# Two-layer graph network on one core: how the experts' gathered rows are turned

## The chip, the core and the metric

The kernel runs on one core of one Trainium2 chip. The metric is the device time of one execution in microseconds (us). The kernel before took 1842.46 us (median of three runs, 1840.32 to 1843.58). The engines are TensorE (PE, whose weight loads are listed apart as PEld), VectorE (DVE), ScalarE (ACT), GpSimd (POOL) and SyncE (SP). Each has an instruction queue of its own, and SP, ACT and POOL also issue DMAs from that queue.

## The reference, cut to what matters

There are N = 3327 nodes with D = 256 features, and a dense 0/1 adjacency matrix. The reference computes four steps, each on a layer norm of the running state `x` and each added to it.

```
x += gat2(layernorm(x), adj)                 # two heads, softmax over neighbours
x += moe(layernorm(x))                       # 16 experts, the best 2 of each node
x += elu(gat1(layernorm(x), adj))            # one head
x += recurrent(layernorm(x))                 # 30 steps: tanh, silu, layernorm, 256x256 matmul

# moe, for a node h and each of its two experts e with weight g_e:
out = sum_e g_e * ((silu(h @ w1[e]) * (h @ w2[e])) @ w3[e])     # w1,w2: 256x512, w3: 512x256
```

All arithmetic is in 32-bit floating point.

## The kernel before, in words

Nodes lie in 26 columns of 128 partitions (`NT` = 26). The program has four stages. First comes the two-head attention, then the experts, then the one-head attention, and last the 30 recurrent steps.

**Attention (`attend`).** The work is cut into parts: a group of columns and a head. The groups of the first attention are columns 0-3, 4-9, 10-15, 16-21 and 22-25, so a part is 512 or 768 wide. For each of the 26 source columns ACT makes `e` (L276), DVE multiplies it by the mask into `pT` (L281), and PE multiplies `pT` with `wh` (L286). `e` and `pT` have three buffers each (pool `edge0`), so ACT and DVE can be a few columns ahead of PE.

**Routing (`route`).** While the next group is being attended to, the finished group is routed in small steps taken from a queue called `later`. DVE measures the rows, POOL takes the power -1/2 (`rstd`, L121), and DVE writes the normalized `row` (L128). One DMA per group, issued from ACT (L516), stores `row` in DRAM as `table_x`. PE transposes `row` in pairs of columns (L148), ACT copies the result out of PSUM (L149), PE makes the gate logits (L526), and DVE picks the two experts and a place in each expert's list (`ati`, L579). POOL then writes the lists with one indirect DMA per column and choice (L592).

**Tiles of the experts.** The lists are cut into tiles of 128 rows of one expert (`find_tiles`). Sixteen tiles are made from the first 16 columns (`FIRST` = 16), and the other 45 once all columns are routed (`ALWAYS` = 61). Tile s uses one of three sets of matrices, number s mod 3. `weights(s)` issues the loads of w1, w2 and w3 from SP (L800 to L802), and skips the transfer if that set already holds the expert. Two of the three sets lie in the memory of `wh`, which becomes free when the attention ends.

**The loop over tiles (`work_off`).** In step s, POOL gathers the rows of tile s+4 from `table_x` by an indirect DMA (L761) into a `rb` buffer that holds three tiles; there are two such buffers, shared with the attention's row factors. PE makes the products with w1 and w2 (L835, `product`), ACT applies silu (L881), DVE multiplies (L885). PE transposes the next tile's rows (`features_first`, L826) and ACT copies them out (L827). Then PE makes the product of tile s-1 with w3 (L851, `results`), DVE weighs it (L854), and POOL scatters it to `given` (L855). The part of the routing that is left over (the group of columns 22-25) runs in the same loop as `aside`.

The order on each engine is fixed when the program is built: a scheduler with its own estimate of times lays the instructions of each engine out in one list. Instructions marked to keep program order are exempt, and so is whatever a dependency ties.

## Time and profile before

| | |
|---|---|
| median of three runs | 1842.46 us (1840.32 to 1843.58) |
| the profiled execution's own time | 1841.14 us |
| its span, first to last instruction | 1839.4 us |
| granted TensorE clock | 0.995 |
| PE busy | 1787.4 us, 97% of the span |
| DVE, ACT, POOL busy | 1319.1, 1223.9 and 888.4 us |
| first attention with the routing, from 92 to 388 us | PE busy 289.9 of 296 us, DMA share 0.45 |
| experts, from 388 to 741 us | PE busy 346.2 of 353 us, DMA share 0.89 |

A line of the timeline gives the start in us, the busy time in us, the engine, the line of the kernel, the operation, output<-inputs and, after x, how many instructions were merged; in brackets stands how long the engine had been idle and who released it. SPq and ACTq are DMAs issued from those queues. In a group line the last fields are the total busy time, the mean of one in ns, and the idle time before. In the answer by stages each engine has its busy time and, in brackets, its instructions, followed by the granted clock, the share of time the DMA engines were busy, and GB/s.

### The profile page before, as it was taken

Reading aid. Unit: us, or ns where it says so; the run is one execution under the profiler, and the core shown is the slowest. Engines: PE = TensorE matmul, PEld = TensorE weight load, DVE = VectorE, ACT = ScalarE, POOL = GpSimd, SP = SyncE. Lnnn points to the kernel's source line nnn. Section 1 sums busy time; section 2 is a strip of 40 time slices with the busy share of each in tenths; the row PEclk is TensorE's granted clock in tenths of the full one; section 3 lists DMA queues with packets and bytes.
Section 4 is the critical chain, followed back from the end, with each engine's and each line's share of the span. In section 5 each row is a group of like instructions: output and inputs, shape, how many; then the busy total and the mean of one; then the engine's idle time right before and its main releaser. Section 6 shows DMA issues by size and latency. Waiting matters only on the chain.

```text
span 1839.4 us, 32502 instructions
## 1 busy us (share of the span) xinstructions
PE 1787.4 (97%) x10980; PEld 1631.7 (89%) x10980; DVE 1319.1 (72%) x4039; ACT 1223.9 (67%) x1587; POOL 888.4 (48%) x654
## 2 busy tenths in 40 slices
PE   7999999999999999799999999999999999999997
PEld 6999999898999999688888878888888888888886
DVE  6888878853222222657677678999999999999998
ACT  2877667642111111366666579999999999999994
POOL 3010212155333332100111028988898889888984
PEclk9999999999999999899999999999999999999999
DMA  8887360258999886400000036666667666666667
GB/s 178 114 123 91 66 101 16 67 187 255 349 345 333 304 301 225 159 9 22 14 18 22 12 84 172 172 172 168 171 167 178 173 172 172 172 167 169 175 172 218
DMA packets 458610, 284.44 MB, mean 155 GB/s; under 512 B 305269, under 2 KB 418220, under 8 KB 458442
## 3 DMA queue, kind: packets, MB, share of 16 engines
q1 hardware_dynamic: 442322, 249.47, 48.4%
q0 software_dynamic: 11440, 28.09, 8.8%
q10 hardware_dynamic: 4680, 4.76, 0.8%
q8 instruction: 90, 1.47, 0.3%
q14 instruction: 78, 0.64, 0.1%
HBM read 168.19 MB, written 91.69 MB: 141 GB/s over the span
## 4 chain that ended last, share of the span: by engine, by line
PE 67%; issue 10%; DVE 6%; POOL 5%; DMA 3%; ACT 1%; another core or an unknown queue 0%; SPq 0%; POOLq 0%; DVEq 0%; ACTq 0%
PE po L1120 35%; PE acc L286 24%; PE bank L1085 4%; DVE pT L281 3%; POOL given L855 2%; POOL rb L761 2%; DMA given<-wh,to 2%; PE bank L835 1%; PE acc L163 1%; PE bank L148 1%; DMA old<-kept 1%; PE bank L526 1%; PE acc L851 1%; DMA lists<-pair,ati 0%; DVE x L1130 0%
## 5 line engine op out<-in xcount | busy, mean ns | idle before, releaser
L276 ACT ACTIVATE e<-rb,minus,full 128x384 f32<-128x384 f32 (+3 forms) x494 | 399.2, 823 | 168.6 <-DVE pT L281 150.8
L1055 POOL TENSOR_TENSOR th<-th,x 128x1024 f32<-128x1024 f32 (+1 forms) x210 | 465.0, 2214 | 94.1 <-ACT th L1052 86.4
L281 DVE SCALAR_TENSOR_TENSOR pT<-e,part,adjT 128x384 f32<-128x384 f32 (+3 forms) x494 | 383.5, 782 | 117.8 <-PE acc L286 101.9
L1120 PE MATMUL po<-wc,adjT 128*128 128x256 f32 x1888 | 422.2, 379 | 0.0
L1120 PEld LDWEIGHTS po<-wc,adjT 128*128 128x128 f32 x1888 | 356.4, 190 | 47.6 <-DVE x L1130 0.3
L1130 DVE SCALAR_TENSOR_TENSOR x<-po,rr,bb 128x256 f32<-128x256 f32 x780 | 325.1, 478 | 61.8 <-PE po L1120 61.2
L286 PE MATMUL acc<-wh,pT 128*128 128x129 f32 x2704 | 311.0, 276 | 2.3 <-DVE pT L281 2.3
L286 PEld LDWEIGHTS acc<-wh,pT 128*128 128x128 f32 x2704 | 305.5, 192 | 3.6 <-DVE pT L281 3.0
L286 PE MATMUL acc<-s_wh,pT 128*128 128x257 f32 x1352 | 295.5, 381 | 3.6 <-DVE pT L281 3.6
L286 PEld LDWEIGHTS acc<-s_wh,pT 128*128 128x128 f32 x1352 | 255.8, 190 | 42.7 <-DVE pT L281 7.0
L1120 PE MATMUL po<-wc,zT 128*128 128x256 f32 x1232 | 281.0, 379 | 0.8 <-DVE x L1130 0.8
L1064 DVE BATCH_NORM_STATS2 stats<-z 128x6 f32<-128x256 f32 x780 | 274.1, 412 | 1.4 <-ACT z L1059 1.4
L1120 PEld LDWEIGHTS po<-wc,zT 128*128 128x128 f32 x1232 | 229.2, 190 | 29.7 <-issue 1.1
L1095 ACT COPY adjT<-z 128x1024 int16<-128x1024 int16 x236 | 235.2, 1044 | 4.8 <-DVE pT L281 2.0
L121 POOL TENSOR_TENSOR rstd<-ve,neg_half 128x4 f32<-128x4 f32 (+3 forms) x28 | 32.0, 1141 | 410.4 <-DVE ve L119 312.3
L1052 ACT ACTIVATE th<-x 128x1024 f32<-128x1024 f32 (+1 forms) x210 | 209.2, 996 | 29.0 <-DVE x L1130 23.8
L1075 POOL TENSOR_TENSOR rr<-rr,neg_half 128x4 f32<-128x4 f32 (+1 forms) x210 | 206.8, 985 | 26.4 <-DVE rr L1070 26.3
L1059 ACT ACTIVATE z<-th 128x1024 f32<-128x1024 f32 (+1 forms) x210 | 207.0, 986 | 7.9 <-POOL th L1055 1.8
L885 DVE TENSOR_TENSOR pT<-e,bank 128x512 f32<-128x512 f32 x61 | 41.9, 688 | 179.7 <-PE bank L835 119.6
L881 ACT ACTIVATE e<-bank 128x512 f32<-128x512 f32 x61 | 36.4, 597 | 196.9 <-PE bank L835 117.2
L835 PEld LDWEIGHTS bank<-hT,wh 128*128 128x128 f32 x1280 | 149.6, 192 | 9.3 <-issue 4.5
L835 PE MATMUL bank<-hT,wh 128*128 128x128 f32 x1280 | 150.6, 276 | 6.5 <-ACT hT L827 2.5
(196 smaller groups left out, 1546.6 us busy)
## 6 DMA issues: line engine op xcount, KB each, us to landing
wh<-in_w_dram SPq DMA_DIRECT2D x120, 512.0 KB
apart<-adjT SPq DMA_DIRECT2D x236, 256.0 KB
first_set<-in_w_dram SPq DMA_DIRECT2D x63, 512.0 KB
in_bytes<-in_adj_dram POOLq DMA_DIRECT2D x3, 2496.0 KB
adjT<-apart SPq DMA_TRANSPOSE x236
x<-in_x_dram SPq DMA_DIRECT2D x6, 512.0 KB
kept<-x SPq DMA_DIRECT2D x8, 384.0 KB
old<-kept SPq DMA_DIRECT2D x6, 512.0 KB
```

The costliest lines, as they stand in the source:

```text
L276: nc.scalar.activation(e[:, : n * P], rb[:, : n * P], AF.Relu, scale=sc.full[:, j, h : h + 1], bias=sc.minus[:, j, h : h + 1],)
L281: masked = nc.vector.scalar_tensor_tensor(pT[:, : n * P], e[:, : n * P], sc.part[:, j, h : h + 1], adjT[:, j // 2, ts[0] * P : (ts[-1] + 1 ...
L286: nc.tensor.matmul(po[c], lhsT=pT[:, c * P : (c + 1) * P], rhs=wh[:, j, h, :], start=(j == 0 and c % per_bank == 0), stop=(j == NT - 1), s ...
L835: nc.tensor.matmul(p[:, f, :], lhsT=w[:, k, f * P : (f + 1) * P], rhs=hT[:, k, :], start=(k == 0), stop=(k == KD - 1),)
L1052: self.put(nc.scalar.activation(self.th, self.hs, AF.Tanh, scale=1.0 / S))
L1055: self.put(nc.gpsimd.tensor_tensor(self.th, self.th, self.hs, ALU.add))
L1059: self.put(nc.scalar.activation(self.z, self.th, AF.Silu, scale=1.0 / S))
L1064: self.put(nc.vector.bn_stats(stats[:, j, :], self.z[:, j, :]))
L1075: self.put(nc.gpsimd.tensor_tensor(r, r, neg_half[:, : self.n], ALU.pow))
L1095: self.put(nc.scalar.copy(parts[:, c : c + 2], halves[:, c : c + 2]))
L1120: nc.tensor.matmul(self.po[:, j, :], lhsT=self.zT(j, k), rhs=wc[:, k, :], start=(k == 0), stop=(k == KD - 1),)
L1130: nc.vector.scalar_tensor_tensor(self.hs[:, j, :], self.po[:, j, :], self.r[:, j : j + 1], bb, op0=ALU.mult, op1=ALU.add)
```

## The change

The gathered rows of a tile are no longer transposed by TensorE. There are four parts.

1. `table_x` holds each row as two planes of 16-bit halves: all low halves, then all high halves. In `route`, ACT copies each pair of columns into such planes (new L524), in a buffer of the attention's `e` ring, and issues one DMA for each pair (new L526): 13 DMAs where there were 5.
2. After the gather (new L774, same size), a tile is written to one of six DRAM buffers `asked` (`put`, new L782), issued from SP for the first three tiles and from ACT for the others. A transposing DMA from SP (`face`, new L786) brings it back with features on the partitions, into one of three `face` buffers. `features_first`, with its two transposes and one copy for each tile, is gone.
3. The matmuls of `product` and `results` (new L864 and L880) are tied to each other in program order by dependencies without semaphores.
4. Numbers of tiles are dealt so that consecutive tiles of one expert go to the same set of matrices, s, s+3, s+6 and so on, where before they went to s, s+1, s+2.

```diff
-    table_x = dram.tile([NP, D], F32, name="table_x")
+    table_x = dram.tile([NP, 2 * D], I16, name="table_x")
@@ route
-            nc.scalar.dma_start(table_x[here, :].rearrange("(t p) d -> p t d", p=P), row[:, :n, :])
+            halves = row.bitcast(I16).rearrange("p j (d b) -> p j b d", b=2)
             for j0 in range(0, n, 2):
+                planes = run.tile([P, MOST * P], F32, name="e").bitcast(I16)[:, : 4 * D]
+                nc.scalar.copy(planes.rearrange("p (j b d) -> p j b d", j=2, b=2), halves[:, j0 : j0 + 2])
+                here = slice((t0 + j0) * P, (t0 + j0 + 2) * P)
+                nc.scalar.dma_start(
+                    table_x[here, :].rearrange("(t p) c -> p t c", p=P), planes.rearrange("p (j c) -> p j c", j=2)
+                )
                 hT = turned(row[:, j0 : j0 + 2, :], turn, ps)
@@ numbers of tiles
-        numbers(two[:, 0, :], [[1, SLOTS]], 0, 0)
+        for s0, n in ((0, FIRST), (FIRST, ALWAYS - FIRST)):
+            no = 0
+            for lane in range(SETS):
+                here = two[:, 0, s0 + lane : s0 + n : SETS]
+                numbers(here, [[1, here.shape[1]]], no, 0)
+                no += here.shape[1]
@@ gathered
+            ahead.append(rows)
+        def put(queue):
+            put_down.append(next(asked))
+            queue.dma_start(put_down[-1], ahead.popleft())
+        def face():
+            hT = faces.tile([P, KD, P], F32, name="face")
+            nc.sync.dma_start(
+                hT.bitcast(I16), put_down.popleft().rearrange("t (b d) -> (t b) d", b=2), transpose=True
+            )
+            facing.append(hT)
@@ product, results: every matmul through behind_latest
+        def behind_latest(ins):
+            nonlocal latest
+            if latest:
+                tc.add_manual_dep(
+                    ins.ins, latest.name,
+                    mybir.DependencyInfo(mybir.DependencyClass.NoSync, mybir.DependencyReason.DATA),
+                    reason="the experts' products in their order",
+                )
+            latest = ins.ins
@@ work_off
-            hT = features_first(ahead.popleft())
+            hT = facing.popleft()
...
                     nc.scalar.activation(act, pa, AF.Silu)
+                    if s + 3 < s1:
+                        put(nc.scalar)
...
-                        hT = features_first(ahead.popleft())
+                        hT = facing.popleft()
                 if s > max(s0, 1):
                     results(s - 1, hidT)
+                if s + 2 < s1:
+                    face()
                 if s + SETS - 1 < s1:
                     weights(s + SETS - 1)
@@ between attention and experts
-        ahead.append(gathered(3))
+        gathered(3)
+        for _ in range(3):
+            put(nc.sync)
+        face()
         weights(1)
+        face()
```

More of the change, by code (lines that the diff above doesn't have):

```diff
@@ L507, in gat_moe_gat_recurrent_ffn @@
         gate = moe.enter_context(tc.tile_pool(name="gate", bufs=1))
+        faces = moe.enter_context(tc.tile_pool(name="faces", bufs=3))
         turn = moe.enter_context(tc.tile_pool(name="turn", bufs=2))
@@ L514, in route @@
             normalized([x[:, t, :] for t in ts], [row[:, j, :] for j in range(n)])
-            here = slice(t0 * P, (t0 + n) * P)
-            nc.scalar.dma_start(table_x[here, :].rearrange("(t p) d -> p t d", p=P), row[:, :n, :])
+            halves = row.bitcast(I16).rearrange("p j (d b) -> p j b d", b=2)
             yield
@@ L613, in route @@
                 for s in range(3):
-                    ahead.append(gathered(s))
+                    gathered(s)
             if ts is groups0[2]:
@@ L650, in gat_moe_gat_recurrent_ffn @@
         two = rec.tile([P, 2, SLOTS], F32, name="prod")
-        numbers(two[:, 0, :], [[1, SLOTS]], 0, 0)
+        for s0, n in ((0, FIRST), (FIRST, ALWAYS - FIRST)):
[4 more added lines that the diff above has]
+                no += here.shape[1]
+        numbers(two[:, 0, ALWAYS:], [[1, SLOTS - ALWAYS]], ALWAYS - FIRST, 0)
         numbers(two[:, 1, :], [[P, SLOTS]], 2 * NP, 1)
@@ L692, in find_tiles @@
             yield
-            tile_no = two[:, 0, :n]
+            tile_no = two[:, 0, here]
             mine = room_m[:E, :, :n]
@@ L753, in find_tiles @@
             nc.vector.tensor_tensor(to[:, here], tof, spare, ALU.add)
-        places = []
+        places, asked = [], cycle([dram.tile([P, 2 * D], I16, name=f"asked{q}") for q in range(6)])
+        ahead, put_down, facing = deque(), deque(), deque()
         def gathered(s):
@@ L759, in gathered @@
                 places.append(rows_p.tile([P, MOST * P], F32, name="rb"))
-            row = places[-1][:, (s % 3) * D : (s % 3 + 1) * D]
+            rows = places[-1].bitcast(I16)[:, (s % 3) * 2 * D : (s % 3 + 1) * 2 * D]
             nc.gpsimd.indirect_dma_start(
-                out=row, out_offset=None, in_=table_x[: EARLY * P, :] if s < FIRST else table_x,
+                out=rows, out_offset=None, in_=table_x[: EARLY * P, :] if s < FIRST else table_x,
                 in_offset=bass.IndirectOffsetOnAxis(ap=which[:, s : s + 1], axis=0),
             )
-            return row
+            ahead.append(rows)
[8 more added lines that the diff above has]
+            facing.append(hT)
         behind = None
@@ L820, in recurrence_parameters @@
                 nc.vector.tensor_scalar(wc[:, k, :], wc[:, k, :], S, None, op0=ALU.mult)
-        def features_first(row):
-            pt = ps_o.tile([P, 512], F32, name="acc0")[:, :D].rearrange("p (k q) -> p k q", k=KD)
-            hT = turn.tile([P, 2, KD, P], F32, name="hT")[:, 0]
-            for k in range(KD):
-                nc.tensor.transpose(pt[:, k, :], row[:, k * P : (k + 1) * P], ident)
-            nc.scalar.copy(hT, pt)
-            return hT
+        latest = None
+        def behind_latest(ins):
[7 more added lines that the diff above has]
+            latest = ins.ins
         def product(hT, w):
@@ L834, in product @@
                 for k in range(KD):
-                    nc.tensor.matmul(
-                        p[:, f, :], lhsT=w[:, k, f * P : (f + 1) * P], rhs=hT[:, k, :],
-                        start=(k == 0), stop=(k == KD - 1),
+                    behind_latest(
+                        nc.tensor.matmul(
+                            p[:, f, :], lhsT=w[:, k, f * P : (f + 1) * P], rhs=hT[:, k, :],
+                            start=(k == 0), stop=(k == KD - 1),
+                        )
                     )
@@ L842, in edge @@
             return run.tile([P, MOST * P], F32, name=name)[:, :HID].rearrange("p (f q) -> p f q", f=FH)
-        ahead = deque()
         def results(s, hidT):
@@ L850, in results @@
             for f in range(FH):
-                nc.tensor.matmul(po, lhsT=hidT[:, f, :], rhs=w3[:, f, :], start=(f == 0), stop=(f == FH - 1))
+                behind_latest(
+                    nc.tensor.matmul(po, lhsT=hidT[:, f, :], rhs=w3[:, f, :], start=(f == 0), stop=(f == FH - 1))
+                )
             y0 = 6 * KD * HID + s % 2 * D
@@ L877, in work_off @@
                     if s + 4 < s1:
-                        ahead.append(gathered(s + 4))
+                        gathered(s + 4)
                     pa = product(hT, ew[s % SETS][0])
@@ L933, in gat_moe_gat_recurrent_ffn @@
         behind = None
+        latest = None
         with tc.If(more > ALWAYS - FIRST):
-            ahead.extend(gathered(s) for s in range(ALWAYS, ALWAYS + 4))
+            for s in range(ALWAYS, ALWAYS + 4):
+                gathered(s)
+            for _ in range(3):
+                put(nc.scalar)
             for s in range(ALWAYS, ALWAYS + SETS - 1):
+                face()
                 weights(s)
```

## The prediction

> **What bounds the kernel now.** I read the page first, then the stages, then single stretches of the timeline. By stages, the two concerned are:

> ```profile
> 92.00:388.00 296.00, 289.90 (x2548) 285.56 (x2547) 247.66 (x519) 212.60 (x233) 64.50 (x53) 1.00 0.45 72
> 388.00:741.00 353.00, 346.15 (x2623) 331.33 (x2621) 86.91 (x209) 62.38 (x126) 128.50 (x130) 1.00 0.89 300
> ```

> The first number after each stage's length is PE's busy time. PE sets the pace in both, 98% busy, so whatever makes it wait lengthens the run. One tile of the experts in the timeline:

> ```profile
> 562.44 3.73 PE L835 MATMUL bank<-hT,wh 128*128 128x128 f32 x32
> 566.01 0.38 PE L826 MATMUL acc<-ident,rb 128*128 128x128 f32 x2
> 566.23 1.89 PE L851 MATMUL acc<-wh,pT 128*128 128x256 f32 x8
> 567.96 3.73 PE L835 MATMUL bank<-hT,first_set 128*128 128x128 f32 x32
> ```

> A tile takes 567.96-562.44 = 5.52 us without a gap. Its two transposes hold PE from 566.01 to 566.23, 0.22 us.

> Now the attention where a group of six columns is routed:

> ```profile
> 187.15 3.03 ACT L276 ACTIVATE e<-rb,minus,full 128x768 f32<-128x768 f32 x3 [1.08 <-DVE pT L281]
> 188.35 1.99 POOL L121 TENSOR_TENSOR rstd<-ve,neg_half 128x6 f32<-128x6 f32 x1 [39.11 <-DVE ve L119]
> 190.37 2.03 DVE L128 TENSOR_SCALAR row<-x,mv,rstd 128x256 f32<-128x256 f32 x6 [1.25 <-POOL rstd L121]
> 190.84 0.76 PE L148 MATMUL bank<-ident,row 128*128 128x128 f32 x4 [0.57 <-DVE row L128]
> ```

> `row` is late for PE by 0.57 us. But ACT had made three more `e` before it, and they carry PE while ACT copies `hT`.

> The last part of the attention, and the hand-over to the experts:

> ```profile
> 369.72 1.58 POOL L592 DMA_INDIRECT lists<-pair,ati  x1 [5.24 <-DVE x L503]
> 370.69 18.03 PE L286 MATMUL acc<-wh,pT 128*128 128x129 f32 x160
> 371.43 13.64 ACT L276 ACTIVATE e<-rb,minus,full 128x512 f32<-128x512 f32 x16
> 389.70 0.99 POOL L761 DMA_INDIRECT rb<-table_x,which  x1 [0.30 <-issue]
> 393.23 1.04 POOL L121 TENSOR_TENSOR rstd<-ve,neg_half 128x4 f32<-128x4 f32 x1
> 395.26 0.94 PE L835 MATMUL bank<-hT,wh 128*128 128x128 f32 x6 [2.53 <-ACT hT L827]
> ```

> ACT's last 16 `e` run without a gap, 0.85 us each; PE's last 20 source columns take 0.90 each. ACT is about four columns ahead.

> For prices of new operations, from the recurrent stage and the lists:

> ```profile
> L1095 ACT COPY adjT<-z 128x1024 int16<-128x1024 int16 x236 | 235.2, 1044 | 4.8 <-DVE pT L281 2.0
> 1213.30 1.31 SPq L1097 DMA_DIRECT2D apart<-adjT  x2
> 1215.78 2.57 SPq L1107 DMA_TRANSPOSE adjT<-apart  x2
> 313.74 0.96 POOL L592 DMA_INDIRECT lists<-pair,ati  x1 [1.72 <-DVE pT L281]
> 316.97 0.34 SPq L667 DMA_DIRECT2D row<-lists  x1
> ```

> A copy into planes of a pair of columns is the same form as L1095, 1.04 us. A write to DRAM lands about 2.1 us after its issue (1213.67 to 1215.78), and an indirect DMA 2.27 us after POOL has done its part (314.70 to 316.97).

> [...] each load from SP (L802) stands until PE's L851 has freed the set, 123 us in all. [...] the trace has a mean of 273, but only 0.11 us from start to start, and this is what can be saved.

> **The change, part by part.** I followed the compiled order of both kernels' instructions on each engine and put the durations above on it.

> *Transposes off PE:* 61 tiles x 0.22 = 13.4 us gained, if nothing else comes to bound the tile. The copies L827 (0.37 us) lie on ACT, which is mostly idle here; their removal gains nothing.

> *Weights dealt by set:* with the reference's inputs, tiles that load a set fall from 57 to 30. At 1.57 MB and some 340 GB/s each load is 4.6 us of the DMA engines. I count nothing for the steady tiles, since PE is already gapless there with nearly all loads. It pays for the new traffic: 0.66 of 200 us for about 63 pairs of a 256 KB write and transpose is 2.1 us a pair in the recurrent stage, so half the size costs at most 1.05 us a tile, against 2.3 saved. If that cover were gone, the tile would go towards the DMA share of 0.99 seen at 500 us, not yet beyond it.

> *The transposing DMA's latency:* `face` is issued two tiles ahead, after the loads of the tile before, so it has 8 to 10 us. SP's work for a tile is 1.24 + 3 x 0.8 = 3.6 us of 5.3. No row shows its landing; from about 2 us (a plain DMA) to 10 it costs nothing, beyond that 1 us a tile each. I take nothing. In the steady loop each `put` stands before silu of the tile six earlier, and its gather was issued long before: also nothing.

> *The ties on PE* only fix the order; in the steady tiles it is the order before.

> *Planes in the routing.* ACT's order has the first copy L524 right behind the last `e` that PE can use before `row`, where before three or four more `e` stood there. ACT thus waits for `row`, and the rings run empty. From the first pair of `row`: copy 1.04, next `e` 1.03, `pT` 1.02, hand-overs 0.2 = 3.3 us, against PE's transposes (0.44) and the rest of its column (0.7): about 2.2 us idle. Then two more `e` come only with two copies and two `hT` copies and more between them: 0.58+1.04+1.03+0.58+1.04+0.58+1.03 = 5.9 us, while PE has two columns (2.7), transposes (0.88) and one set of gate logits (0.8): 1.5 to 2.2 idle. Less the 0.6 to 0.8 that PE loses now, a group of six columns costs 3.9, the group of four 2.5, and the group routed beside the 512-wide part, where stocks are smaller but less is moved, about 2.6: 2.5 + 2 x 3.9 + 2.6 = 12.9 us. From below, if the ring covered all of it, 0; from above, if planes hold buffers of the ring for 4 to 5 us because DMA is busy (0.45 on average here), 20.

> *Puts on ACT.* The order has the puts of tiles 3 to 8 among the last 16 `e` of the attention. Tile 3's gather stands on POOL behind six list writes. These can start some 3 us earlier than now (the step that makes `ati` stands four `pT` earlier), at about 366.7; six take 10.3 us (369.72 to 380.01), then the gather 1.2 and its landing 2.3: 380.5. ACT gets to this put at about 371.4 and waits 9 us, and behind it stand the 16 `e`. PE has 3.4 us of stock, and after the wait needs 1.7 until the next `pT`: some 7 us idle. Six more list writes stand before tile 6's gather: 1.5 more. Together 8.5; at best 3, if list writes run at 1.27, at worst 13.

> *Hand-over.* Six gathers, not three, now stand on POOL before the last group's `rstd`, and the silu product of tile 0 stands on DVE behind that `row`; PE's results of tile 0 are tied before product 1. So PE waits about 4.9 us where it now loses 2.5. Before each set of gate logits it waits for a copy (0.9 together), and tile 10's `face` stands before its weights behind the wait for the lists. Against that, two waits of 2.3 and 1.7 us (at 435 and 455 us), in the stretch where DMA is full, should shrink. I take +2.3, from -4 to +6.

> Sum: -13.4 + 12.9 + 8.5 + 2.3 = +10.3 us. On the profiled execution's 1841.1 (span 1839.4 and 1.7 around it) this is 1851.4; the median of the runs is 1.3 above it, so 1853 us.

> **Rivals.**
> 1. *The stocks hold* (faster). If `e` and `pT` carry PE over the copies and puts, what stays is -13.4 and some 4 us of waits for DMA: 1825 to 1832. It decides when ACT's new waits cost PE less than about 10 us in all. For it: ACT is busy only 213 of 296 us, and idles for free buffers (59 us on `pT`). Against it: the order, which makes ACT wait in front of the `e` that are needed. 0.12.
> 2. *Even*: the waits are as told but at their low ends (about 6 in the routing, 4 for the puts, less than nothing at the hand-over): 1839 to 1846. 0.14.
> 3. *The turned rows come late* (slower still): a transpose that lands after 11 us where 10 are there adds 1 us to some 45 tiles: 1870 to 1900. For it: no row shows the landing; three DMAs in a chain (gather, put, face). Against it: the DMA engines are relieved. 0.11.
> 4. *The favourite*, 0.63: 1843 to 1866.

> That the change fails to do what it says is excluded on PE's side, whose compiled order has no transposes left in the tiles.

> **How the numbers follow.** A run tells a difference from 0.2% (3.7 us) on. Faster: rival 1 and nothing else, 0.12. Within: half of rival 2, 0.07. Slower: the rest, 0.81. The range 1840 to 1868 leaves out rival 1 and most of rival 3. The favourite alone spans 1843 to 1866, from the ends of its four terms taken together as partly independent.

> **What would show it.** Steady tiles at 5.30 us start to start, with no PE wait for `face`. In the first attention, PE's busy time the same but the stage 20 us longer, with waits of 2 to 3 us for `pT` just after each `row` and one of 5 to 8 us some 16 `e` before its end, and ACT idle there until POOL's gather has landed. First product of the experts near 410 us, not 388. DMA share of the experts well below 0.89. The prediction is wrong if the attention ends before 400 us, if the steady tile isn't 5.2 to 5.4 us, or if PE waits for `face` in most tiles.

## The result and the profile after

The kernel with the change takes 1894.01 us (median of six runs, 1885.45 to 1897.75), the kernel before 1842.01 us on the same chip (six runs, 1839.63 to 1843.58). The ratio is 1.0277, with a 95% interval from 1.0252 to 1.0302. It is slower, as predicted, but by 52 us instead of 11, and it lies 26 us above the upper end of the predicted range.

The profiled execution of the changed kernel took 1888.65 us with a span of 1885.8, so it is 5 us quicker than the median. Against the profiled execution of before (span 1839.4) it is 46.4 us longer. Three marks cut this up: the first product of the experts, the first matmul after them (L136 in both), and the end.

| stretch | before | after | difference |
|---|---|---|---|
| start to the first product of the experts | 388.56 | 428.08 | +39.5 |
| first product to L136 | 353.96 | 359.34 | +5.4 |
| L136 to the end | 1096.9 | 1098.4 | +1.5 |

The answer by stages for the changed kernel, with PE's busy time behind each stage's length, and ahead of the last two fields (DMA share, GB/s) the granted clock:

```profile
92.00:388.00 296.00, 275.81 (x2283) 272.07 (x2283) 223.99 (x467) 197.45 (x213) 43.08 (x39) 0.94 0.44 71
388.00:428.00 40.00, 31.88 (x262) 31.32 (x261) 24.72 (x52) 23.35 (x30) 25.13 (x22) 0.91 0.34 70
428.00:788.00 360.00, 339.91 (x2501) 320.74 (x2500) 86.80 (x209) 42.16 (x69) 122.32 (x122) 0.98 0.79 215
```

The first two rows together are the attention, 336 us where before it was 296. PE's work is the same (2283 + 262 = 2545 instructions, 2548 before), but two things have grown. PE is idle for 336 - 307.69 = 28.3 us, where it was 6.1. And PE is *busy* for 307.7 us where it was 289.9, 17.8 us longer for the same matmuls. The clock, 0.94 and 0.91 instead of 1.00, says why. The page shows it in one group of matmuls, whose mean was 276 ns before:

```profile
L286 PE MATMUL acc<-wh,pT 128*128 128x129 f32 x2704 | 323.9, 283 | 24.8 <-DVE pT L281 16.7
```

Cut into windows of 0.5 us from 0 to 1880 us, this trace has a clock of 1.00 in 3604 windows, of 0.50 in 130, and a value between in 26. Four-microsecond windows beside one of the new gaps (377 to 379 us):

```profile
380.00:384.00 4.00, 4.00 (x20) 4.00 (x20) 2.65 (x7) 2.78 (x5) 0.00 (x0) 0.50 0.00 0
384.00:388.00 4.00, 4.00 (x35) 4.00 (x34) 3.39 (x10) 3.17 (x5) 0.00 (x0) 0.92 0.00 0
```

In the first of them PE is busy for all of its 4 us and gets through 20 matmuls, against 38 at a clock of 1.00 (130 to 134 us). So from here on I count two losses, from windows of 2 us: the *idle* time of PE, and the *clock loss*, its busy time times (1 - granted clock). The last column is the kernel before in the stretches where it does the same work (for the groups 108-135, 185-225, 262-292 and 336-362 us).

| stretch after | idle / clock loss, us | the same work before |
|---|---|---|
| four routed groups (108-136, 192-232, 280-312, 360-388) | 20.1 / 16.9 | 5.3 / 0 |
| puts at the end of the attention (400-428) | 8.1 / 2.1 | 0 / 0 |
| rest of the attention | 0.1 / 0 | 0.8 / 0 |
| experts (428-788) | 20.1 / 4.8 | 8.4 / 1.7 |

The gaps of the attention are where the prediction put them. The timeline at the first group, in order of time, with DMA issues as SPq and ACTq:

```profile
111.56 1.05 ACT L524 COPY e<-row 128x1024 int16<-128x1024 int16 x1 [5.60 <-DVE row L128]
114.64 0.95 PE L286 MATMUL acc<-wh,pT 128*128 128x129 f32 x4 [2.46 <-DVE pT L281]
117.88 8.30 SPq L335 DMA_TRANSPOSE adjT<-in_bytes  x4
123.02 0.59 ACT L149 COPY hT<-bank 128x512 f32<-128x512 f32 x1 [7.13 <-DMA adjT<-in_bytes]
```

ACT stands idle for `row` in front of the first copy, then copy and `e` follow, and PE waits 2.46 us for `pT`: forecast 2.2. The rest is new to me: ACT stood idle for 6.7 us, from 115.88 us to its second write of planes at 122.58, and its work behind the write waited too. The profile puts this wait down to SP's transposing DMAs of another tensor.

The same at the end of the attention:

```profile
409.42 2.93 ACT L276 ACTIVATE e<-rb,minus,full 128x512 f32<-128x512 f32 x4 [9.56 <-DMA rb<-table_x,which]
411.07 13.92 PE L286 MATMUL acc<-wh,pT 128*128 128x129 f32 x104 [7.94 <-issue]
```

ACT, whose next instruction is a put (issued at 408.98 us), waits 9.56 us for a gather to land (forecast 9), the `e` behind it start at 409.42, and PE waits 7.94 (forecast some 7, and 1.5 more later).

A steady tile of the experts:

```profile
601.21 3.73 PE L864 MATMUL bank<-face,first_set 128*128 128x128 f32 x32
...
606.50 1.72 PE L864 MATMUL bank<-face,wh 128*128 128x128 f32 x14
```

It takes 606.50 - 601.21 = 5.29 us, where it was 5.52. But PE has waits of over 1 us between the first product and L136; these, and two of 1.66 (a load) and 1.79 us (a turned tile):

```profile
436.61 3.78 PE L880 MATMUL acc<-first_set,pT 128*128 128x256 f32 x8 [4.80 <-DVE pT L917]
489.91 3.81 PE L864 MATMUL bank<-face,first_set 128*128 128x128 f32 x32 [1.47 <-DMA first_set<-in_w_dram]
519.00 3.81 PE L864 MATMUL bank<-face,wh 128*128 128x128 f32 x32 [3.08 <-DMA face<-asked]
537.24 5.44 PE L864 MATMUL bank<-face,wh 128*128 128x128 f32 x32 [2.10 <-DMA wh<-in_w_dram]
```

The first is the hand-over, at 4.8 us against a forecast of 4.9. The others wait for loads and turned rows, between 468 and 596 us. Before, PE had no gap at all there (40.00 us busy in each 40), at a DMA share of 0.95 to 1.00.

### The profile page after: what moved, and what is told of

Its sections match the earlier page's. It is cut to its first block, busy times and chain, and to the rows that moved or that the text cites. A ratio compares the mean times of both kernels' runs of the same rounds, so it can differ in the third digit from the quotient of the medians.

```text
span 1885.8 us, 32324 instructions
## 1 busy us (share of the span) xinstructions
PE 1802.1 (96%) x10858; PEld 1641.7 (87%) x10858; DVE 1322.8 (70%) x4039; ACT 1212.4 (64%) x1539; POOL 885.6 (47%) x660
## 4 chain that ended last, share of the span: by engine, by line
PE 53%; DVE 2%; DMA 1%; POOL 1%; ACT 1%; issue 0%; SPq 0%; ACTq 0%; DVEq 0%; POOLq 0%
PE po L1163 34%; PE acc L286 14%; PE bank L1128 3%; DVE pT L281 1%; PE acc L163 1%; DMA th<-given 1%; DMA old<-kept 0%; POOL th L1098 0%; ACT adjT L1138 0%; POOL rstd L121 0%; DVE x L1013 0%; DVE low L1047 0%; DVE x L1181 0%; ACT s_wh L1028 0%; DVE x L1173 0%
## 5 line engine op out<-in xcount | busy, mean ns | idle before, releaser
L276 ACT ACTIVATE e<-rb,minus,full 128x384 f32<-128x384 f32 (+3 forms) x494 | 398.6, 823 | 181.1 <-DVE pT L281 154.2
L281 DVE SCALAR_TENSOR_TENSOR pT<-e,part,adjT 128x384 f32<-128x384 f32 (+3 forms) x494 | 384.3, 783 | 145.3 <-PE acc L286 109.7
L1163 PEld LDWEIGHTS po<-wc,adjT 128*128 128x128 f32 x1888 | 356.4, 190 | 47.5 <-DVE x L1173 0.3
L286 PE MATMUL acc<-wh,pT 128*128 128x129 f32 x2704 | 323.9, 283 | 24.8 <-DVE pT L281 16.7
L286 PEld LDWEIGHTS acc<-wh,pT 128*128 128x128 f32 x2704 | 318.1, 199 | 26.7 <-DVE pT L281 18.3
L286 PE MATMUL acc<-s_wh,pT 128*128 128x257 f32 x1352 | 297.1, 382 | 4.0 <-DVE pT L281 4.0
L286 PEld LDWEIGHTS acc<-s_wh,pT 128*128 128x128 f32 x1352 | 257.0, 191 | 43.5 <-DVE pT L281 7.3
L1107 DVE BATCH_NORM_STATS2 stats<-z 128x6 f32<-128x256 f32 x780 | 274.1, 412 | 1.4 <-ACT z L1102 1.4
L1138 ACT COPY adjT<-z 128x1024 int16<-128x1024 int16 x236 | 235.2, 1044 | 4.8 <-DVE pT L281 2.0
L911 ACT ACTIVATE e<-bank 128x512 f32<-128x512 f32 x61 | 36.4, 597 | 305.2 <-PE bank L864 235.2
L1095 ACT ACTIVATE th<-x 128x1024 f32<-128x1024 f32 (+1 forms) x210 | 209.1, 996 | 28.4 <-DVE x L1173 22.5
L121 POOL TENSOR_TENSOR rstd<-ve,neg_half 128x4 f32<-128x4 f32 (+3 forms) x28 | 29.7, 1061 | 410.4 <-DVE ve L119 308.4
L864 PEld LDWEIGHTS bank<-face,wh 128*128 128x128 f32 x1280 | 151.7, 195 | 15.8 <-issue 13.1
L864 PE MATMUL bank<-face,wh 128*128 128x128 f32 x1280 | 154.5, 279 | 10.5 <-DMA face<-asked 5.1
```

What stands on the lines that cost most here:

```text
L276: nc.scalar.activation(e[:, : n * P], rb[:, : n * P], AF.Relu, scale=sc.full[:, j, h : h + 1], bias=sc.minus[:, j, h : h + 1],)
L281: masked = nc.vector.scalar_tensor_tensor(pT[:, : n * P], e[:, : n * P], sc.part[:, j, h : h + 1], adjT[:, j // 2, ts[0] * P : (ts[-1] + 1 ...
L286: nc.tensor.matmul(po[c], lhsT=pT[:, c * P : (c + 1) * P], rhs=wh[:, j, h, :], start=(j == 0 and c % per_bank == 0), stop=(j == NT - 1), s ...
L864: nc.tensor.matmul(p[:, f, :], lhsT=w[:, k, f * P : (f + 1) * P], rhs=hT[:, k, :], start=(k == 0), stop=(k == KD - 1),)
L1095: self.put(nc.scalar.activation(self.th, self.hs, AF.Tanh, scale=1.0 / S))
L1107: self.put(nc.vector.bn_stats(stats[:, j, :], self.z[:, j, :]))
```

## The experiments

Two accounts stood against each other at first. In one, PE's idle time in the attention (ACT's copies, its writes, its puts) is the whole cost, and only its size was forecast too low. In the other, each gap costs a second time, through the halved clock behind it. A third question was where the 13.4 us in the experts went. Each expectation was written before its run; a letter in it is its own name for one of the accounts of that time. Kernels in one batch share the runs of the kernel before, so the ratios are the numbers to compare; the profiles are of one execution each.

**1. The planes alone.** The kernel before, with ACT's copies and the writes added. The writes go to a table that nothing reads, and TensorE still turns the tiles; the old write of `row` remains too.

```diff
+    spare_x = dram.tile([NP, 2 * D], I16, name="spare_x")
...
+                planes = run.tile([P, MOST * P], F32, name="e").bitcast(I16)[:, : 4 * D]
+                nc.scalar.copy(planes..., halves[:, j0 : j0 + 2])
+                nc.scalar.dma_start(spare_x[there, :]..., planes...)
                 hT = turned(row[:, j0 : j0 + 2, :], turn, ps)
```

> The kernel before with one part of the change alone: in each group's routing ACT copies pairs of row into 16-bit planes in the ring of e and writes them to a table that nobody reads; gathers, transposes on TensorE, the order of the tiles are those before. Theory A (each stall of TensorE is paid twice: as idle time and then as time at half clock): the first product of the experts starts 30 to 36 us later than 388.6, of it about 17 us more idle and 17 us at the lowered clock; granted clock of the first attention about 0.95; time 1872 to 1880. Rival B (the lowered clock has to do with the transposing DMAs or the experts' new traffic, not with the stalls): only the idle time, clock 1.00, time 1855 to 1861. Rival C (the puts at the end of the attention are what matters): under 1850.

Measured: 1891.56 us, ratio 1.0263 (1.0246 to 1.0281), slower than all three forecasts. The first product comes at 441.9 us, 53 us later than in the kernel before, and the experts after it take 353.6 us, as before. The attention has 29.8 us of idle time and 30.2 of clock loss: the second account, and as large as the first. That the total comes near the change's own loss is chance, for the attention alone lost 39.5 us there. The first group's timeline shows why it is more here: ACT's wait for the same DMAs again, 9.96 us where it was 7.13 in the changed kernel, with PE waiting 11.04 us where it waited 1.25.

```profile
123.21 0.58 ACT L149 COPY hT<-bank 128x512 f32<-128x512 f32 x1 [9.96 <-DMA adjT<-in_bytes]
123.85 1.89 PE L534 MATMUL bank<-gate_w,hT 128*128 128x16 f32 x8 [11.04 <-ACT hT L149]
```

**2. The dealing alone.** The kernel before with only the tile numbers dealt by set.

```diff
-        numbers(two[:, 0, :], [[1, SLOTS]], 0, 0)
+        for s0, n in ((0, FIRST), (FIRST, ALWAYS - FIRST)):
+            no = 0
+            for lane in range(SETS):
+                here = two[:, 0, s0 + lane : s0 + n : SETS]
...
```

> The kernel before with only the tile numbers dealt by set of matrices. Theory A: fewer loads, DMA share of the experts falls from 0.89 to about 0.6; TensorE is gapless there anyway, so only the two waits near 435 and 455 us (4.0 us together) can go: 1838 to 1842. Rival (the order of the tiles itself costs, for the first sixteen tiles need as many loads in less time): 1844 to 1850.

Measured: 1840.35 us, ratio 0.9988 (0.9979 to 0.9997). The DMA engines' share in the experts falls from 0.89 to 0.55 and the time by 2 us. Loads that are hidden already are worth little, as assumed.

**3 and 4. The planes from POOL; and the puts from SP too.** In the changed kernel, POOL copies one column at a time into the `face` buffers and writes it from its own queue (the last group stays on ACT). The second kernel also issues the puts from tile 3 on from SP.

```diff
-                nc.scalar.copy(planes..., halves[:, j0 : j0 + 2])
-                nc.scalar.dma_start(table_x[here, :]..., planes...)
+                for j in range(j0, j0 + 2) if ts is not groups0[-1] else ():
+                    planes = faces.tile([P, KD, P], F32, name="face")...bitcast(I16)
+                    nc.gpsimd.tensor_copy(planes..., halves[:, j])
+                    nc.gpsimd.dma_start(table_x[(t0 + j) * P : (t0 + j + 1) * P, :], planes)
...
 # fourth kernel only
-                        put(nc.scalar)
+                        put(nc.sync)
```

> The changed kernel with the planes of all groups but the last copied by POOL, one column at a time, in buffers of face, and written from POOL's queue, so that ACT has the order of before in the routing. Theory A: the stalls after each row go, with the low clock behind them: 34 us less than the changed kernel, 1857 to 1864; the stall of about 8 us at the end of the attention, with ACT's puts behind the gathers, stays. Rival B (the low clock has another cause): 17 us less, 1875 to 1880. Rival D (the chain of gather, put and transposing DMA is what costs): within 5 us of 1894.

> As the run before it, and the puts of tiles 3 and later issued by SP instead of ACT. Theory A: the stall of 8 us and 2 us of low clock behind it at the end of the attention go too: 1846 to 1855; what is left against the kernel before is the experts' stage, some 5 us longer by its waits for DMA. Rival E (SP, which now waits for gathers in front of the loads and the transposing DMAs, makes TensorE wait for those): attention ends at 390 to 396 us, but the stage of the experts grows by 10 us or more: 1858 to 1875.

Measured: 1870.71 us, ratio 1.0164 (1.0146 to 1.0181), and 1868.17, ratio 1.0153 (1.0124 to 1.0183). The stages of the first of the two:

```profile
92.00:364.00 272.00, 264.18 (x2310) 259.05 (x2309) 232.98 (x465) 190.94 (x205) 74.99 (x84) 1.00 0.48 77
364.00:408.00 44.00, 33.56 (x238) 31.45 (x238) 23.60 (x55) 21.53 (x28) 25.53 (x24) 0.81 0.25 70
```

With the copies off ACT the attention up to 364 us is nearly what it was: 7.8 us idle (5.6 in the kernel before), clock 1.00. The last stretch has 10.4 idle and 5.4 of clock loss in the third kernel, and 10.7 and 6.8 in the fourth. There the compiled order had moved part of tile 0's first product in among the attention's last columns (it starts at 374 us), and PE waited for `pT` between them. That is a new wait that came with the edit. So neither run reached theory A's time, and the two price the copies, not the puts.

**5. The copies without any write.** The kernel before, plus ACT's copies, whose result is not read.

```diff
+                planes = run.tile([P, MOST * P], F32, name="e").bitcast(I16)[:, : 4 * D]
+                nc.scalar.copy(planes..., halves[:, j0 : j0 + 2])
                 hT = turned(row[:, j0 : j0 + 2, :], turn, ps)
```

> The kernel before with the copies into planes alone: ACT makes them in the ring of e as in the changed kernel, nothing is written from them and nothing reads them. Theory A (the place of the copies in ACT's order makes the stalls, each paid as idle time and again at half clock): groups two to four lose 12 to 13 us each as in the run with planes and writes, the first group 5 to 7 and not 17, because no write stands in ACT's queue behind the transposing DMAs: 1874 to 1886. Rival F (the writes from ACT's queue, which wait in front of the next e, make the stalls): 1842 to 1855.

Measured: 1861.01 us beside 1835.40, ratio 1.0126 (1.0106 to 1.0147). So the copies in ACT's order cost 25.6 us, and the writes in ACT's queue cost the other 23 of the first experiment, where both the old write and the new ones stand. This lies between the two forecasts: each named a part of the cause. The first product comes at 409.7 us. The attention has 12.6 idle and 16.6 clock loss. One group's windows:

```profile
192.00:196.00 4.00, 1.84 (x9) 1.84 (x10) 1.30 (x2) 2.47 (x4) 0.00 (x0) 0.80 0.86 271
196.00:200.00 4.00, 4.00 (x21) 3.82 (x19) 0.00 (x0) 0.59 (x2) 0.00 (x0) 0.50 0.12 41
200.00:204.00 4.00, 3.91 (x19) 3.77 (x18) 1.73 (x2) 4.00 (x5) 0.00 (x0) 0.50 0.02 4
```

One gap of 2.68 us (191.5 to 194.2) is followed by half clock from 194.4 to 211.5 us.

**6. The puts from SP.** The changed kernel with only the puts from tile 3 on moved to SP (the one-word edit shown above).

> The changed kernel with the puts of tiles 3 and later issued by SP, the planes left on ACT. Theory A: of the changed kernel's stall after 400 us 8.1 us of idle time and 2.1 us of low clock go: 1882 to 1887. Rival E (the wait only moves, since SP waits in front of the transposing DMAs and the loads): 1890 to 1900.

Measured: 1881.98 us, ratio 1.0248 (1.0231 to 1.0265). The end of its attention:

```profile
388.00:418.00 30.00, 30.00 (x269) 29.88 (x268) 25.75 (x55) 24.61 (x31) 20.93 (x17) 1.00 0.32 72
```

PE has no gap there, and the first product comes at 418.1 us instead of 428.1. So the puts cost 10 us there, 8.1 idle and 2.1 at half clock. But the experts take 7.4 us more (366.7). SP now waits for gathers in front of the puts (it issues nothing from 401.47 to 409.51 us, when the first of these puts goes out), and the loads and turned rows stand behind them. The largest new wait of PE is at the hand-over, 13.3 us where it was 4.80. A good part of the stall moved, though the time comes near the one that theory A forecast. If the parts add up, an estimate for the writes in the changed kernel's attention follows: 39.5 us less 21.2 for the copies (409.7 - 388.56 in run 5) and 10 for the puts leaves some 8.

**7. The tiles not dealt.** The changed kernel with tiles numbered as before.

> The changed kernel with the tile numbers in the order of before. Theory A: 57 loads of 4.6 us of the DMA engines and 61 times some 1.5 us for gather, put and turned rows beyond what they were make about 5.8 us of DMA a tile, against 5.3 of TensorE: the stage of the experts becomes bound by DMA and 10 to 35 us longer: 1904 to 1930. Rival (the loads stay hidden, as the dealing alone brought 2 us to the kernel before): 1894 to 1898.

Measured: 1935.63 us, ratio 1.0537 (1.0517 to 1.0557). The steady part of the experts:

```profile
604.00:764.00 160.00, 140.42 (x995) 128.44 (x994) 28.59 (x49) 14.93 (x25) 48.69 (x50) 0.98 1.08 315
```

The DMA share is 1.08, where the changed kernel has 0.69 in the same window, and PE is idle 19.6 us of 160 (0.9 there); the experts take 406.8 us, 47.5 more, and the run is slower than both forecasts. The dealing, worth 2 us on its own, is worth about 48 us here (ratio 1.0537 instead of 1.0277). My reading of these shares is that the new traffic needs the room that the dealing makes. These two parts of the change can't be priced one at a time.

**8, 10 and 11. Planes made after the gather.** `table_x` stays in floats, so the attention is left alone, and ACT splits each gathered tile in the experts' stage before its put. The first tiles are turned by TensorE as before: 6 in runs 8 and 10, 16 in run 11. In runs 10 and 11 the copies are also tied behind silu on ACT, and the parameter loads go from POOL.

```diff
+            planes = ... # one tile, in an hT buffer (runs 10 and 11: in an e buffer)
+            halves = ahead.pop(s).bitcast(I16).rearrange("p (d b) -> p b d", b=2)
+            nc.scalar.copy(planes.rearrange("p (b d) -> p b d", b=2), halves)
             put_down.append(next(asked))
-            queue.dma_start(put_down[-1], ahead.popleft())
+            queue.dma_start(put_down[-1], planes)
...
-                        hT = facing.popleft()
+                        hT = facing.popleft() if s + 1 >= EARLIEST else features_first(s + 1)
```

> A version that keeps the turned rows but takes the planes out of the attention: the table is float as before, ACT splits a tile's gathered rows into planes in the experts' stage, where it is mostly idle, and then puts them down; tiles 0 to 5 are turned by TensorE as before; dealing and ties as in the changed kernel. Theory A: attention as before, ending at 388 us with the clock at 1.00; 55 x 0.22 = 12.1 us saved on TensorE, less waits for DMA of 0 to 8 us: 1827 to 1840. Rival G (the chain of four steps comes late, or the transposing DMAs hold up the loads, so that TensorE waits in most tiles): 1842 to 1870.

> As the version that splits planes after the gather, with three things mended: ACT's copies tied behind the silu of three tiles before, so that no copy that waits for a gather stands in front of a silu that is due; planes in the ring of e instead of the hT ring of the last group's routing; the loads of the next layer's parameters from POOL's queue and not in front of ACT's puts. Tiles from 6 on are turned by DMA. Theory A: 0.990 to 0.998 of the kernel before. Rival G (DMA: gather, put and turned rows take some 2.5 us of the DMA engines a tile, and in the stretch with the loads TensorE still waits): 1.000 to 1.008.

> The same with the first sixteen tiles, whose stretch is full of loads, turned by TensorE as before; the 45 others by DMA. Theory A: 45 x 0.22 = 9.9 us off TensorE and 2 us from the dealing, less 0 to 4 us of waits: 0.993 to 0.998 of the kernel before. Rival G: waits for turned rows or loads in the remaining tiles eat it up: 0.999 to 1.005.

Measured: ratios 1.0149 (1.0132 to 1.0166), 1.0049 (1.0032 to 1.0066) and 1.0037 (1.0023 to 1.0052). The first product comes at 386.4, 387.3 and 387.0 us, so the 39.5 us of the attention are gone with the planes and puts in it. The experts take 371.8, 366.2 and 357.9 us, against 354 before. All three lie in rival G's range. In run 8 the compiled order put two of ACT's copies ahead of a silu that was due, and ACT stood 13.06 us for a gather at 456 us. In run 10 that wait is gone; ties, buffers and the queue of the parameter loads changed together there, so it isn't shown which of them did it. What remains in runs 10 and 11 are waits of 2 to 5 us for gathers, ACT and loads, in run 11 up to 507 us and in run 10 up to 618.

**9. The gap filled.** Run 5 plus 14 unread matmuls on PE right behind each group's first transposes, where the gap is.

```diff
+                if j0 == 0:
+                    fill = bank()
+                    for q in range(14):
+                        nc.tensor.matmul(fill[:, :P], lhsT=ident, rhs=row[:, q % 2, :P], start=True, stop=True)
```

> The run with the copies alone, and 14 matmuls of 128 columns that nobody reads, put behind the first transposes of each group, where TensorE stood idle for 2.7 us in front of the half clock: 14 x 0.11 = 1.5 us of work in the gap. Theory A (the idle gap is what halves the clock): no or nearly no time at half clock in the groups (16.6 us of loss before), although TensorE does more: 10 to 18 us faster than the copies alone, which stood at 1.0126 of the kernel before, so 1.003 to 1.007 of it. Rival H (the clock falls for a reason other than the gap, as heat or DMA load): low clock as there, and the added work only costs: 1.012 to 1.017.

Measured: 1863.07 us, ratio 1.0122 (1.0105 to 1.0139), the same as run 5. The filler, meant to take 1.5 us, takes 3.29 (its 14 matmuls stand as 28 in the records, 0.12 us each), so it can't win time, and the time lies in rival H's range. The clock is what decides between the two. The windows that answer to those of run 5:

```profile
192.00:196.00 4.00, 4.00 (x37) 3.88 (x37) 2.39 (x6) 3.84 (x5) 0.00 (x0) 1.00 0.86 239
196.00:200.00 4.00, 4.00 (x38) 4.00 (x37) 1.02 (x1) 3.02 (x5) 0.00 (x0) 1.00 0.37 129
200.00:204.00 4.00, 2.72 (x21) 2.63 (x22) 2.07 (x4) 3.09 (x4) 0.00 (x0) 0.85 0.00 0
```

Same copies on ACT, the same transposes, no gap on PE, and the clock stays at 1.00. In this group it falls only behind the gap that is left, of 1.28 us at 201.9. The filler does two things at once, though: it takes the idle time away, and it adds matmuls. Which of these the clock answers to is not shown. In the whole attention the clock loss falls from 16.6 to 2.9 us and the idle time from 12.6 to 6.6. The first product comes at 403.0 us instead of 409.7, although PE has some 13 us more to do before it. The experts give it back (361.4 instead of 353.7 us): the last group's filler lies there, and a load is waited for 4.2 us.

**12 and 13. The ties.** The kernel before with its products tied in order, and the changed kernel without ties.

```diff
 # run 12, each matmul of product and results
-                    nc.tensor.matmul(
+                    behind_latest(nc.tensor.matmul(
...
 # run 13
-            if latest:
+            if False:
```

> The kernel before with only the ties that keep the experts' products and results in order. Theory A: the steady order is the same, and at the hand-over the results of tile 0 stand in front of the second product and wait for the silu product behind row: 0 to 3 us slower, 1.000 to 1.002. Rival (the ties make the 4.8 us wait seen in the changed kernel at 432 us, with low clock behind it): 1.002 to 1.005.

> The changed kernel without the ties on the experts' products. The experts' stage of the changed kernel, from first product to the first matmul after it, took 359.3 us where 343 had been forecast. Theory I (the ties make the wait of 4.8 us for the silu product at the hand-over and the low clock behind it): stage 3 to 8 us shorter, ratio to the kernel before 1.023 to 1.026. Theory II or III (the cause is in the steady part): stage within 2 us, 1.027 to 1.029.

Measured: 1843.38 us, ratio 1.0019 (1.0013 to 1.0026), and 1937.56, ratio 1.0535 (1.0516 to 1.0553). PE in a steady tile of the changed kernel without ties:

```profile
603.43 3.73 PE L864 MATMUL bank<-face,wh 128*128 128x128 f32 x32
...
608.01 1.99 PE L880 MATMUL acc<-wh,pT 128*128 128x256 f32 x8 [0.42 <-DVE pT L917]
609.85 3.73 PE L864 MATMUL bank<-face,wh 128*128 128x128 f32 x32
```

Without ties each tile's results stand directly behind its own product, and PE waits for that tile's `pT`: this tile takes 6.42 us instead of 5.29, and in the whole stage PE waits 48.4 us for `pT`. Neither forecast of run 13 had this. My reading, which no run tests, is that the transposes used to stand there and gave the scheduler something to put between. Ties cost some 3 us in the kernel before and save about 48 in the changed one (1.0535 instead of 1.0277).

**14 and 15. The turned rows on ACT's queue.** `face` is issued from ACT instead of SP: in the changed kernel, and in run 11's, there without ties and right behind the put of the next tile.

```diff
-            nc.sync.dma_start(
+            nc.scalar.dma_start(
                 hT.bitcast(I16), put_down.popleft()..., transpose=True
```

> The changed kernel with the transposing DMAs of the turned rows in ACT's queue in place of SP's. Theory II (on SP they stand in front of the loads of the matrices, and make these late): the waits for the loads in the steady part, about 6 us and the low clock behind them, go: 1.022 to 1.026. Theory III (the DMA engines' own time for gather, put and turned rows is the cause): no shorter, 1.027 to 1.032, for ACT then also waits for puts to land.

> The version with sixteen tiles turned by TensorE and 45 by DMA, with the transposing DMAs in ACT's queue behind the put of the next tile, and without the ties of the products. If ties (3.5 us by themselves) and the place in SP's queue were what kept it at 1.0037 of the kernel before: 0.994 to 0.999. If the DMA engines' time is the limit: 1.000 to 1.003.

Measured: ratios 1.0393 (1.0374 to 1.0413) and 1.0139 (1.0119 to 1.0159), both worse than with `face` on SP and than all forecasts. In run 14 ACT stands idle for 5.28, 7.19 and 4.27 us in front of the silus at 567, 575 and 580 us; the profile puts 111.3 us of such waits in all down to `face`. Run 15 changes three things at once, so it gives no price of the queue alone.

**16, 17 and 18. The best of what was learned.** Run 16 turns tiles 0 to 21 by TensorE, without ties, and 22 to 60 by DMA, tied. Run 17 also issues SP's loads ahead of `face`. Run 18 is run 16 with the six DRAM buffers laid into the memory of `in_bytes`.

```diff
-        EARLIEST = 16
+        EARLIEST = 22
...
-            if latest:
+            if latest and tied:      # tied: from step 20 on
...
 # run 17
-                if EARLIEST <= s + 2 < s1:
-                    face()
                 if s + SETS - 1 < s1:
                     weights(s + SETS - 1)
+                if EARLIEST <= s + 2 < s1:
+                    face()
```

> The version that splits planes after the gather, with tiles 0 to 21 turned by TensorE and untied, and the 39 from 22 on turned by DMA and tied: the hand-over and the stretch full of loads are left as before. If the ties at the hand-over (3.5 us) and the waits for loads near 506 us (4.7 us and the low clock behind them) were what ate the gain: 39 x 0.22 = 8.6 us and 2.2 us from the dealing, less 2 to 5 us of waits: 0.996 to 0.998 of the kernel before. If the DMA engines' time is the limit in the steady part too: 0.999 to 1.003.

> The same with SP's loads in front of the turned rows of the tile. If the transposing DMA in front holds up the loads: 1 to 3 us faster than the run before it. If the turned rows then come late: slower, with waits of TensorE for face.

> The version with tiles from 22 on turned by DMA, its six buffers in DRAM laid into in_bytes, which is idle by then, in place of 0.75 MB of their own; the order of instructions on every engine is the same as there. In that run the experts' stage was 7 us shorter than in the kernel before, but the recurrent stage, whose instructions stand in the same order in both, 6 us longer, and its DMA share 0.71 to 0.68. Theory J (the added buffers move the recurrent stage's own buffers to other DRAM addresses, where its transposing DMAs take longer): recurrent stage back at 1095 to 1099 us, 0.996 to 0.998 of the kernel before. Rival (something the experts leave behind, or chance): 1101 to 1104 us there, 1.000 to 1.002.

Measured: 1839.30 us beside 1837.16, ratio 1.0014 (1.0005 to 1.0024); 1863.58, ratio 1.0134 (1.0118 to 1.0150); and 1839.34 beside 1835.99, ratio 1.0016 (1.0008 to 1.0025). All that follows the experts in run 16:

```profile
733.00:1836.00 1103.00, 1076.42 (x5263) 942.74 (x5263) 923.04 (x3099) 899.28 (x1143) 676.72 (x437) 0.99 0.52 130
```

Its experts take 347.0 us (386.1 to 733.1), 7 less than before: 39 tiles at 0.22 are 8.6 us, and PE's busy time there falls by 7.2 (338.4 against 345.6) while its idle time stays (8.5 against 8.4). So the ratio lies in the range of the DMA limit, but not for that reason: the stages behind the experts take 1103 us instead of 1096.9. PE's idle time there is 2.5 us longer and its busy time 3.7, of which the clock loss is 2.2. The order of instructions in them is the same in both kernels. Run 18 tried one reason, other DRAM addresses, and it fell: 1103.2 us again. Runs 3 and 4 have such long stages too (1102.1 and 1103.6 us). Why stays open. In run 17 `face` stands behind the loads, and PE waits 9.8 us for it where it waited for none in run 16, so rival 3 of the prediction is real once `face` loses its place in the queue.

No version with turned rows by DMA beats the kernel before. The dealing alone is the fastest that was run, at 0.9988.

## Why the prediction was right or wrong, point by point

The miss is 36.1 us (46.4 between the profiled executions against 10.3): 18.1 in the attention (39.5 against 12.9 + 8.5), 16.5 in the experts (+5.4 against -13.4 + 2.3), and 1.5 behind them. Two steps failed.

**Transposes off PE, -13.4: the mechanism right, the sum not reached.** A transpose (L826) has a mean of 273 ns in the records of before, but the two of a tile hold PE for 0.22 us, and the steady tile went from 5.52 to 5.29 us. Of the stage, PE's busy time fell by only 6.3 us (345.6 to 339.3): the clock loss grew by 3.1 us (1.7 to 4.8), and some 4 us I can't place.

**Planes in the routing, +12.9: the gaps right in place and near in size, but more than half of the loss missed.** The stall after the first pair of `row` was forecast at 2.2 us and is 2.46 to 2.68 in the first three groups; the next, forecast at 1.5 to 2.2, is 2.73 in the second and third. Net of what the same work lost before, the groups of four, six, six and six columns were forecast at 2.5, 3.9, 3.9 and 2.6 us of gaps and have 3.4, 4.6, 4.7 and 2.1, 14.8 together. The 3.9 itself was more than its terms give: 2.2 and 1.5 to 2.2, less 0.6 to 0.8, are 2.9 to 3.8. In the first group, 1.25 us is a wait that I did not have at all, behind ACT's second write. Beside the gaps come 16.9 us of clock loss.

**Puts on ACT, +8.5: right, but for the clock.** 8.1 us of idle time, 2.1 of clock loss, and run 6 prices the whole at 10.

These two terms were 21.4 us together and the attention's idle time grew by 22.2. **The first step that failed is the sum itself**: it took each microsecond that PE waits as one microsecond, with "PE's busy time the same". It grew by 17.8 us. In run 9, with the same copies and the gap filled with matmuls, the clock stays at 1.00 from 192 to 200 us, where run 5 has 0.80 and 0.50. The trace of before had an instance that I overlooked, behind its only gap in that stretch, the 2.53 us of the hand-over (a window of the kernel before):

```profile
396.00:400.00 4.00, 4.00 (x16) 3.41 (x15) 0.82 (x3) 0.00 (x0) 1.91 (x2) 0.57 1.06 376
```

The price could be read there: 4 us of PE at 0.57 is 1.7 us lost beside 2.5 of gap. But the same trace had gaps of 2.34 and 1.68 us (at 435 and 455 us) with full clock behind them, so it would have given a risk and no fixed price.

**Hand-over, +2.3: the wait right, the relief wrong. This is the second step that failed.** The wait is 4.8 us against 4.9. But PE's idle time in the experts grew by 11.7 us where +2.3 was forecast. The "two waits [...] in the stretch where DMA is full" that "should shrink" went the other way: they were 4.0 us, and the waits for loads and turned rows became 11.4 (6.3 and 5.1). Two of my terms lie under it. The new traffic was put at 1.05 us of the DMA engines a tile at most. The queues' shares from 596 to 690 us, of before and then of after, give its price:

```profile
q1 hardware_dynamic: 16104, 23.65, 75.0%
```

```profile
q1 hardware_dynamic: 16133, 11.81, 44.2%
...
q10 hardware_dynamic: 2447, 2.23, 9.1%
```

Before, 0.75 x 94 us for 15 loads is 4.7 us a load, as forecast (4.6, from some 340 GB/s; the kernel before moves 344 GB/s from 468 to 508 us). After, 6 loads leave 13.3 us of q1 for 18 turned rows, 0.74 each, if a load takes as long as before; q10 has 17 puts at 0.50; and a gather with its scatter rises from 0.76 to 1.04 (q0, from 13.8% for 17 to 19.9% for 18). That is 1.5 us a tile, so the DMA share fell only to 0.79, not "well below 0.89". Between 468 and 596 us, where many tiles still load, it stands at 0.9. And I took nothing for a late `face`, which cost 5.1 us in three places. That loads come late because `face` stands in front of them on SP is read from the order only; run 17, which put them first in another kernel, lost more on `face` than it won.

**The rivals.** Rival 1 (the stocks hold) is out: its limit was 10 us of waits, and the attention alone lost 39.5. That the time lies in the range of rival 3 (turned rows late) is chance: PE waits for `face` three times, not in most tiles. The mark "PE waits for `face` in most tiles" did not come true, nor did the attention end before 400. The marks for the steady tile, the waits after each `row` and the stall before the end did. "Near 410" for the first product was 428.

The difference between the stages' sum (46.4 us) and the medians (52) is not explained by one profiled execution. It was among the quickest of its six.

## What to carry to other kernels

In the attention here PE's new gaps were paid about twice, once as the gap (22 us) and once through the half clock behind it (19 us). In the experts most gaps cost only themselves (20.1 us idle, 4.8 of clock loss). So in a stage that PE bounds, look at the granted clock in windows of 2 to 4 us behind each gap of the kernel before, and put a second cost, as a risk, beside the price of every wait that a change adds. Work that is moved off the bounding engine onto an idle one (ACT here) is not free if it stands in front of what feeds the bounding engine: look at the order, not at the busy share. And price combined edits together: the dealing was worth 2 us alone and 48 in this company, the ties -3 and +48.
